# An edge matrix counted in blocks of 32 destinations and a quarter of the sources, in place of 64 and a half

## The chip, the cores and the metric

The kernel runs on one core of a Trainium2 chip. The metric is the device time of one launch in microseconds (us), the median of several runs.

## What is computed

A graph has N = 6250 nodes with 128 features, and E = 100,000 edges (`src`, `dst`, one of 8 types), sorted by `dst`. Two graph networks follow each other, each with its input added and a layer norm behind it:

```python
# three relational layers: messages by edge type, mean over each (node, type)
seg = dst * R + etype
agg = segment_sum(h[src, etype] / max(cnt[seg], 1), dst)
x = agg + x @ root + bias            # then batch norm and relu, but for the last
# then a light graph network on the same edges (row = src, col = dst)
h = x @ W_in + b_in
edge_weight = deg_inv_sqrt[row] * deg_inv_sqrt[col]
for _ in range(3):
    cur = segment_sum(cur[col] * edge_weight[:, None], row)
    acc = acc + cur
final = (acc / 4) @ W_out + b_out
```

The second network needs, three times, the product of the matrix A (how many edges lead from each source to each destination) with a 6250 x 64 matrix. A does not depend on features, so the kernel counts it while the relational layers run.

## The kernel before, in words

**The first network.** For each layer l the kernel makes a table `h_d` of transformed nodes (L975, L976, L977) and walks the edges in tiles of 128. One tile of one layer is a *slot*: POOL gathers 128 rows by an indirect DMA (L1857, out of `x_d` for 100 tiles and out of `h_d` for 462), and PE multiplies them with a small one-hot block (L1860) into a bank that DVE adds to `agg` (L1908) or `z` (L1878). There are `SLOTS` = 562 slots in a layer. A gather has 19 buffers. Destinations with very many edges go another way, `dense` (L1510, L1514, with their loads at L1381 and L1401 and their unpacking at L1423 and L1425).

**What sets the order.** All work beside the slots is written as Python generators. `streams` gives each generator a stretch of slots, and at each slot every stream is advanced in proportion: it emits its instructions until its next `yield`. The order of PE and DVE is taken as emitted (`tc.manual_schedule`); each engine runs its own list in order and waits by semaphores. SP issues nearly all the DMAs, in its own order. In layer 0 run the counts of the busiest destinations (`hot_counts`), `dense` and, from slot 300 to 502, `tables`; in layers 1 and 2 run `dense`, `degrees` and one half each of `counts`.

**Tables.** The edge tiles lie in a grid of 98 rows by 8 tiles. A *step* takes TS = 4 neighbouring tiles (a half row) and one *block* of BD = 64 destinations. Since edges are sorted, each half row is used by one block or by a few neighbouring ones, so there are NST = 196 + 98 = 294 steps for any input. `tables` finds out which block and which half row each step has: comparisons of the blocks' edges with the first and last destination of each half row (L1613, L1615), their sums by matmul (L1623, L1632), masks over all steps (L1639 to L1644), five fp32 matmuls of 294 columns that spread the results over the partitions (L1660), and sixteen that select the steps' sources and destinations (L1675). The tables `e_src`, `rel_s`, `e_val` (128 x 1176, fp32) hold for each edge of each step its column, its row and its value. `step_i` holds the block of each step and whether it is the block's last; `keep` is 0 at a block's first step.

**Counts.** S = 896 sources of seven *fields* share one int32 word by different bits (e_val is a power of two per field), so A needs 896 words a destination. The upper half of these columns is put on other partitions: the 128 partitions of a sum are 64 destinations x 2 halves, with SH = 448 columns each. For every step, over 4 yields and with the matmuls 6 yields behind,
- DVE makes one one-hot block `dst_hot` of 4 x 128 columns (L1732, three buffers),
- DVE makes for each tile a `row` of 448 columns, which holds the edge's value at its column (L1736),
- PE sums `dst_hot` x `row` over the four tiles in one PSUM bank (L1742),
- DVE adds it to the running sum of the block, `had` (L1714, four buffers),
- SP reads block and last-flag into registers, eight steps at a time (L1718), and stores `had` into `a_d` if the step is the block's last (L1723, a conditional DMA of 224 KB, `[block][partition][column]`).

**The last stage** (from about 2710 us) loads `a_d` back (L2109), unpacks the fields with DVE (L2117, L2120) and multiplies with PE (L2128, 7203 matmuls of 193 columns).

Of the kernel before, what the change touches and what calls it, by code (L numbers as in the profile page):

```python
# [17 lines left out]
P = 128  # L18
EPS = 1e-5
REGS = 8  # L20
# [499 lines left out]
def sorted_path(  # L520
# [93 lines left out]
    TS = 4  # L614
    BD = P // 2
    NBD = NP // BD
    SH = S // 2
    FAR = 1 << 14
    NG4 = Q * J // TS
    NST = NG4 + NBD  # L620
    LEAD = 6
# [9 lines left out]
    assert 3 * PART + SUB * R + 3 * P <= NP and 9 * SP * R + R * D <= HD * R and CH * 3 * D <= 3 * SUB * R * 2 and 3 * SUB * R <= PART  # L631
# [3 lines left out]
    assert 96 < Q <= P and N + P <= PAD and NBLK % CH == 0 and NBLK == NF * NSL and J == 2 * TS and NST <= 512 and NBD <= P and SR <= SH and LAG < TS  # L635
# [435 lines left out]
    a_d = dram.tile([NBD, P, SH], I32, name="a_d")  # L1071
# [3 lines left out]
    nc.gpsimd.iota(iota_h.rearrange("p (d q) -> p d q", q=2), pattern=[[1, BD], [FAR, 2]], base=0,  # L1075
                   channel_multiplier=0, allow_small_or_imprecise_dtypes=True)
    iota_s = kp.tile([P, NST], F32, name="iota_s")
    nc.gpsimd.iota(iota_s, pattern=[[1, NST]], base=0, channel_multiplier=0,
                   allow_small_or_imprecise_dtypes=True)
    iota_q = kp.tile([P, 1], F32, name="iota_q")  # L1080
    nc.gpsimd.iota(iota_q, pattern=[[0, 1]], base=0, channel_multiplier=2,
# [33 lines left out]
    def near(minus, n):  # L1115

        far = cp.tile([P, TS, P], BF16, name="lo_far")
        hot = cp.tile([P, TS, P], BF16, name="lo_hot", bufs=4)
        for j in range(n):
            nc.scalar.activation(far[:, j, :], iota_f, AF.Abs, bias=minus[:, j : j + 1])  # L1120
        nc.scalar.activation(hot[:, :n, :], far[:, :n, :], AF.Relu, bias=ones[:, 0:1], scale=-1.0)  # L1121
        return hot
# [431 lines left out]
    NGD = -(-NTS // TS)  # L1554

    def degrees():
        DT = 32
        made, summed = [], []
        for y in range(2 * NGD + 4):
            g = y // 2  # L1560
            if y % 2 == 0 and g < NGD:
                t0 = g * TS
                n, k = min(TS, NTS - t0), t0 % DT
# [8 lines left out]
                far = cp.tile([P, TS, NBLK], BF16, name="blk_far", bufs=1)  # L1572
                blk = cp.tile([P, TS, NBLK], BF16, name="blk_hot", bufs=3)
# [28 lines left out]
    step_i = kp.tile([1, 2, NST], I32, name="step_i")  # L1602
    keep = kp.tile([P, NST], F32, name="keep")

    def tables():

        B = NBD
        edge = kp.tile([P, B], F32, name="edge")
        nc.vector.tensor_scalar(edge, iota_f[:, :B], float(BD), None, op0=OP.mult)
        d_in = dst_f[:, 1 : W + 1]  # L1610
        below = flat(e_val)[:Q, : 4 * B].rearrange("p (h k b) -> p h k b", h=2, k=2)
        for h in range(2):
            nc.vector.tensor_scalar(below[:, h, 0], edge[:Q, :], d_in[:, h * 512 + 511 : h * 512 + 512], None,  # L1613
                                    op0=OP.is_gt)
            nc.vector.tensor_scalar(below[:, h, 1], edge[:Q, :], float(BD), d_in[:, h * 512 : h * 512 + 1],  # L1615
                                    op0=OP.add, op1=OP.is_gt)
# [3 lines left out]
        p_t = [ps_w.tile([P, 512], F32, name="pw")[:B, :1] for _ in range(2)]  # L1620
        for h in range(2):
            for k in range(2):
                nc.tensor.matmul(p_t[k], below[:, h, k], ones[:Q, :1], start=(h == 0), stop=(h == 1))  # L1623
        yield
        col = kp.tile([B, 8], F32, name="col")
        t0, n, incl, s0, delta, top = (col[:, i : i + 1] for i in range(6))
        nc.vector.tensor_copy(t0, p_t[0])
        nc.vector.tensor_tensor(n, p_t[1], t0, op=OP.subtract)
        nc.vector.tensor_scalar_max(n, n, 1.0)
        yield  # L1630
        p_i = ps_w.tile([P, 512], F32, name="pw")[:B, :1]
        nc.tensor.matmul(p_i, upto, n, start=True, stop=True)  # L1632
# [5 lines left out]
        past, within, start_, ends = (flat(e_val)[:B, i * NST : (i + 1) * NST] for i in range(4))  # L1638
        nc.vector.tensor_scalar(past, iota_s[:B, :], incl, None, op0=OP.is_ge)  # L1639
        nc.vector.tensor_scalar(within, iota_s[:B, :], s0, None, op0=OP.is_ge)  # L1640
        yield
        nc.vector.tensor_sub(within, within, past)
        nc.vector.tensor_scalar(start_, iota_s[:B, :], s0, None, op0=OP.is_equal)
        nc.vector.tensor_scalar(ends, iota_s[:B, :], top, None, op0=OP.is_equal)  # L1644
        delta_b = kp.tile([B, P], F32, name="delta_b")
        nc.vector.tensor_copy(delta_b, delta.to_broadcast([B, P]))
        step_b = kp.tile([P, NST], F32, name="step_b")
        step_g = kp.tile([P, NST], F32, name="step_g")
        made = (
            (ones[:B, :], past, lambda p: nc.vector.tensor_scalar(step_b, p[:, :NST], float(BD), None, op0=OP.mult)),  # L1650
            (delta_b, within, lambda p: nc.vector.tensor_add(step_g, p[:, :NST], iota_s)),
            (ones[:B, :], start_, lambda p: nc.vector.tensor_scalar(keep, p[:, :NST], -1.0, 1.0, op0=OP.mult,
                                                                    op1=OP.add)),
            (iota_p[:B, :], ends, lambda p: nc.vector.tensor_copy(step_i[:, 0, :], p[:1, :NST])),
            (ones[:B, :1], ends, lambda p: nc.vector.tensor_copy(step_i[:, 1, :], p[:1, :NST])),
        )
        yield
        for of, by, take in made:
            p = ps_w.tile([P, 512], F32, name="pw")
            nc.tensor.matmul(p[: of.shape[1], :NST], of, by, start=True, stop=True)  # L1660
            yield
            take(p)

        sel = [flat(rel_s)[:Q, h * NST : (h + 1) * NST] for h in range(2)]
        for h in range(2):
            nc.vector.tensor_scalar(sel[h], step_g[:Q, :], float(h), iota_q[:Q, :], op0=OP.subtract,
                                    op1=OP.is_equal)
        yield
        e_key = e_src.bitcast(I32)
        for to, of in ((e_key, key_f), (e_rel, d_in)):  # L1670
            for j in range(TS):
                pe = ps_w.tile([P, 512], F32, name="pw")
                for h in range(2):
                    c = h * 512 + j * P
                    nc.tensor.matmul(pe[:, :NST], of[:, c : c + P], sel[h], start=(h == 0), stop=(h == 1))  # L1675
                yield
                nc.vector.tensor_copy(to[:, :, j], pe[:, :NST])
# [22 lines left out]
        nc.vector.tensor_scalar(upper, e_src, float(SH), None, op0=OP.is_ge)  # L1700
        nc.vector.scalar_tensor_tensor(e_src, upper, -float(SH), e_src, op0=OP.mult, op1=OP.add)
# [3 lines left out]
    def counts():  # L1705

        had = ac.tile([P, SH], I32, name="had")
        nc.vector.memset(had, 0)
        at, runs, ending = {}, [had], []
        rows, hots, sums = {}, {}, {}  # L1710

        def leave(s):
            now = ac.tile([P, SH], I32, name="had")
            nc.vector.scalar_tensor_tensor(now, runs.pop(), keep[:, s : s + 1], sums.pop(s)[:, :SH],  # L1714
                                           op0=OP.mult, op1=OP.add)
            if s % REGS == 0:
                for k, top_ in ((0, NBD - 1), (1, 1)):
                    _, v = nc.values_load_multi_w_load_instructions(  # L1718
                        step_i[0:1, k, s : min(s + REGS, NST)], engines=[ET.SP], min_val=0, max_val=top_,
# [7 lines left out]
        for i in range(NST * TS + LEAD + LAG):  # L1727
            s, j = divmod(i, TS)
            if s < NST:
# [484 lines left out]
```

## Time and profile before

| | |
|---|---|
| median of 3 runs | 3420.43 us (3415.64 to 3430.69) |
| profiled execution | 3407.57 us, of which the span of its instructions is 3405.8 us |
| layer 0 | 0 to about 970 us |
| layer 1, first half of the counts | 971 to 1845 us |
| layer 2, second half of the counts | 1859 to 2706 us |
| last stage | 2709 to 3406 us |
| L1742, 1176 matmuls | 433.8 us busy, 352 ns in the median record |
| L1736, 1176 rows | 451.5 us busy, 402 ns in the mean |
| L1732, 294 one-hot blocks | 202.0 us busy, 687 ns in the mean |
| L1714, 294 running sums | 197.6 us busy, 672 ns in the mean |
| tables, on DVE | 588 to 878 us |

The profile is of one execution. *Busy* is the time in which an engine had at least one instruction of the group under way; matmuls overlap, so a matmul's record is longer than the time by which it holds back the next one. PE is the matmul engine, PEld its weight loads, DVE the vector engine, ACT the scalar engine, POOL the one that issues the gathers, SP the one that issues most DMAs. PEclk is the share of full clock that PE was granted. *Idle before* is the engine's idle time just before the instructions of a group, with what ended it. The *chain* is followed back from the last instruction, at each step to what released it or to the instruction before it on its engine. "issue" is time in which the engine waited for nothing that the profile shows.

### The profile page before, as it was taken

The numbers are of one execution on the slowest core, as the hardware profiler recorded it, in microseconds if no ns is written. First come the engines' busy times: TensorE is split into PE (matmuls) and PEld (weight loads), VectorE is DVE, ScalarE is ACT, GpSimd is POOL, SyncE is SP. The second block draws the span as 40 slices with busy tenths as digits, with TensorE's granted clock in tenths as the row PEclk, the third lists the DMA queues.
The fourth block names the chain that finished last, engine by engine and source line by source line (L and its number), as shares of the span: only waits on it lengthen the run. The fifth ranks groups of instructions, "written<-read, shape, count | busy, mean of one in ns | idle before, by whom it ended". The sixth has DMA issues, their size and how long they took to land.

```text
span 3405.8 us, 57451 instructions
## 1 busy us (share of the span) xinstructions
PE 2833.0 (83%) x19147; PEld 2016.1 (59%) x19147; DVE 2301.2 (68%) x6139; ACT 1121.1 (33%) x3086; POOL 1793.6 (53%) x1703
## 2 busy tenths in 40 slices
PE   5876488889859788878875888888888789999998
PEld 3444355555535455555544455555565589999997
DVE  5977787356547786766776567767667695655665
ACT  3565452000025644353443464535354020000000
POOL 4466666677756777676764667777777500000000
PEclk9876589899869889988996999988988799999998
DMA  6433376555547354554553665545555534443331
GB/s 202 181 110 76 96 215 202 205 177 185 184 140 266 110 191 153 171 182 150 172 174 92 234 220 163 189 153 201 167 173 171 159 89 115 115 115 113 111 104 34
DMA packets 378371, 532.85 MB, mean 156 GB/s; under 512 B 99892, under 2 KB 296674, under 8 KB 378064
## 3 DMA queue, kind: packets, MB, share of 16 engines
q1 hardware_dynamic: 315668, 414.87, 36.9%
q0 software_dynamic: 53952, 110.60, 11.3%
q10 hardware_dynamic: 8444, 3.61, 0.4%
q8 instruction: 152, 2.49, 0.3%
q14 instruction: 155, 1.27, 0.1%
HBM read 390.36 MB, written 205.60 MB: 175 GB/s over the span
## 4 chain that ended last, share of the span: by engine, by line
PE 61%; DVE 11%; issue 8%; another core or an unknown queue 2%; DMA 2%; ACT 2%; DVEq 0%; SPq 0%; POOL 0%; ACTq 0%
PE pw L2128 17%; PE pd L1510 14%; PE ps L1860 7%; PE pw L1742 6%; PE pd L975 5%; PE pd L1514 5%; DVE row L1736 2%; PE pw L1457 1%; DVE had L1714 1%; DVE agg L1908 1%; DVE dst_hot L1732 1%; DMA xT<-c_d 1%; PE pw L1540 1%; PE ps L2078 1%
## 5 line engine op out<-in xcount | busy, mean ns | idle before, releaser
L1857 POOL DMA_INDIRECT gt<-h_d,gidx x1386 | 1468.5, 1060 | 637.0 <-issue 276.3
L1510 PE MATMUL pd<-xT,hs 128*128 128x512 fp8e3 x2646 | 970.5, 421 | 68.1 <-issue 50.4
L1860 PEld LDWEIGHTS ps<-o,gt 128*128 128x128 f32 x3372 | 670.8, 215 | 432.2 <-issue 212.2
L1860 PE MATMUL ps<-o,gt 128*128 128x48 f32 (+1 forms) x3372 | 617.8, 271 | 218.4 <-issue 103.1
L2128 PE MATMUL pw<-three,u 128*128 128x193 bf16 x7203 | 613.5, 248 | 11.7 <-DVE three L2045 9.8
L2128 PEld LDWEIGHTS <-u 128*128 128x128 fp8e3 x7203 | 602.8, 98 | 17.4 <-issue 9.8
L1514 PE MATMUL pd<-xT,hs 128*128 128x256 fp8e3 x1764 | 517.0, 293 | 36.8 <-issue 30.4
L1736 DVE TENSOR_SCALAR row<-iota_c,e_tab,e_tab 128x448 bf16<-128x448 int16 x1176 | 451.5, 402 | 77.6 <-remote 24.1
L1510 PEld LDWEIGHTS <-hs 128*128 128x128 bf16 x2646 | 299.1, 118 | 311.7 <-issue 143.2
L1742 PE MATMUL pw<-row,dst_hot 128*128 128x448 bf16 x1176 | 433.8, 381 | 18.6 <-issue 14.9
L1732 DVE TENSOR_TENSOR dst_hot<-iota_h,e_tab 128x512 bf16<-128x512 f32 x294 | 202.0, 687 | 237.4 <-PE ps L1860 83.7
L975 PE MATMUL pd<-w,xT 128*128 128x512 f32 x588 | 300.8, 636 | 25.7 <-issue 24.7
L1857 POOL DMA_INDIRECT gt<-x_d,xidx x200 | 205.3, 1026 | 144.9 <-PE pw L1742 35.5
L1121 ACT ACTIVATE lo_hot<-lo_far,ones 128x512 bf16<-128x512 bf16 (+1 forms) x370 | 225.3, 611 | 148.4 <-PE pw L1277 69.1
L1575 ACT ACTIVATE blk_far<-iota_f,src_blk 128x49 bf16<-128x49 f32 x782 | 211.4, 324 | 157.6 <-DVE src_blk L1567 71.3
L1576 ACT ACTIVATE blk_hot<-blk_far,ones 128x196 bf16<-128x196 bf16 x196 | 88.1, 449 | 511.3 <-PE ps L1860 213.3
L1120 ACT ACTIVATE lo_far<-iota_f,src_lo 128x128 bf16<-128x128 f32 x782 | 254.7, 387 | 0.1
L1514 PEld LDWEIGHTS <-hs 128*128 128x128 bf16 x1764 | 203.4, 115 | 82.1 <-issue 53.3
L976 ACT COPY hs<-pd 128x512 f32<-128x512 f32 x294 | 171.3, 585 | 221.8 <-PE pd L975 114.9
L1742 PEld LDWEIGHTS <-dst_hot 128*128 128x128 bf16 x1176 | 146.1, 125 | 126.8 <-issue 76.3
L2120 DVE TENSOR_SCALAR u<-packed 128x896 int32<-128x896 int32 x147 | 91.5, 622 | 185.1 <-PE pw L2128 182.7
L1714 DVE SCALAR_TENSOR_TENSOR had<-had,keep,pw 128x448 int32<-128x448 int32 x294 | 197.6, 672 | 3.7 <-PE pw L1742 1.4
(405 smaller groups left out, 2912.9 us busy)
## 6 DMA issues: line engine op xcount, KB each, us to landing
xT<-c_d SPq DMA_DIRECT2D x126, 896.0 KB
h_d<-hs SPq DMA_DIRECT2D x147, 512.0 KB
hs<-p_d SPq DMA_DIRECT2D x105, 672.0 KB
a_d<-had SPq DMA_DIRECT2D x294, 224.0 KB
packed<-a_d SPq DMA_DIRECT2D x147, 448.0 KB
c_d<-had SPq DMA_DIRECT2D x174, 196.0 KB
gt<-h_d,gidx POOLq DMA_INDIRECT x1386
p_d<-hs SPq DMA_DIRECT2D x21, 672.0 KB
```

Source lines behind the costliest of these rows:

```text
L975: nc.tensor.matmul(ph, xT[:, b * P : (b + 1) * P], w[:, c : c + 512], start=True, stop=True)
L1120: nc.scalar.activation(far[:, j, :], iota_f, AF.Abs, bias=minus[:, j : j + 1])
L1121: nc.scalar.activation(hot[:, :n, :], far[:, :n, :], AF.Relu, bias=ones[:, 0:1], scale=-1.0)
L1510: nc.tensor.matmul(sums[0], x3s[n_][:, b, p, :], of[:, :, b, :, :2].rearrange("p s r y -> p y s r"), start=first_, stop=last)
L1514: nc.tensor.matmul(sums[1][:, :HALF], x3s[n_][:, b, p, :], of[:, :, b, :, 2], start=first_, stop=last)
L1714: nc.vector.scalar_tensor_tensor(now, runs.pop(), keep[:, s : s + 1], sums.pop(s)[:, :SH], op0=OP.mult, op1=OP.add)
L1732: nc.vector.tensor_tensor(hots[s], iota_h[:, None, :].to_broadcast([P, TS, P]), rel_s[:, s, :, None].to_broadcast([P, TS, P]), op=OP.is_equal)
L1736: nc.vector.tensor_scalar(rows[i], iota_c, e_src[:, s, j : j + 1], e_val[:, s, j : j + 1], op0=OP.is_equal, op1=OP.mult)
L1742: nc.tensor.matmul(sums[s][:, :SH], hots[s][:, j, :], rows.pop(i - LEAD), start=(j == 0), stop=(j == TS - 1))
L1857: nc.gpsimd.indirect_dma_start(out=gt, out_offset=None, in_=table, in_offset=bass.IndirectOffsetOnAxis(ap=at[:, t : t + 1], axis=0))
L1860: nc.tensor.matmul(pa, gt, columns(t), start=first_, stop=last)
L2128: nc.tensor.matmul(out_of(f), bytes_[WHERE[f][0]][:, d, :, WHERE[f][1]], cur[:, order[c0 + d], :], start=(c0 + d == 0 and f == f0), stop=( ...
```

## The change

A step takes TS = 2 tiles instead of 4, and a block BD = 32 destinations instead of 64. The 128 partitions of a sum are 32 destinations x 4 quarters of the 896 columns, with SQ = 224 columns each. So NG4 = 392, NBD = 196, and NST = 588 steps of two tiles: the tiles of all steps stay 1176. TQ = 4 tiles, that is two steps, share one one-hot instruction and one PSUM bank (2 x 224 columns); each step has its own running sum, conditional store and flags. [...] `a_d` becomes `[196][128][224]`; its words lie where they lay before. `iota_s` has 294 columns, buffers of `row` and `had` keep their size, and 224 of their columns are used. `near` and `degrees` use TQ in place of TS and stay as they are.

```diff
-    TS = 4
-    BD = P // 2
+    TQ = 4
+    TS = 2
+    BD = P // 4
     NBD = NP // BD
+    NBG = NBD // 2
     SH = S // 2
+    SQ = S // 4
     NG4 = Q * J // TS
     NST = NG4 + NBD
+    NSH = NST // 2
+    NSUP = NST * TS // TQ
...
-    a_d = dram.tile([NBD, P, SH], I32, name="a_d")
+    a_d = dram.tile([NBD, P, SQ], I32, name="a_d")
...
-    nc.gpsimd.iota(iota_h.rearrange("p (d q) -> p d q", q=2), pattern=[[1, BD], [FAR, 2]], base=0,
+    nc.gpsimd.iota(iota_h.rearrange("p (d q) -> p d q", q=4), pattern=[[1, BD], [FAR, 4]], base=0,
...
     def tables():
-        B = NBD
+        B, PER = NBG, W // (TS * P)
...
+        for g in range(2):
+            past, within, start_, ends = masks[g]
+            one = lambda v: v[:, g : g + 1]
+            nc.vector.tensor_scalar(past, many[:B], one(incl), None, op0=OP.is_ge)
+            nc.vector.tensor_scalar(within, many[:B], one(s0), None, op0=OP.is_ge)
+            nc.vector.tensor_scalar(start_, many[:B], one(s0), None, op0=OP.is_equal)
+            yield
+            nc.vector.tensor_sub(within, within, past)
+            nc.vector.tensor_scalar(ends, many[:B], one(top), None, op0=OP.is_equal)
+            nc.vector.tensor_copy(delta_b[:, g], one(delta).to_broadcast([B, P]))
+            yield
...
         for of, by, take in made:
-            p = ps_w.tile([P, 512], F32, name="pw")
-            nc.tensor.matmul(p[: of.shape[1], :NST], of, by, start=True, stop=True)
-            yield
-            take(p)
+            for c in (slice(0, NSH), slice(NSH, NST)):
+                p = ps_w.tile([P, 512], F32, name="pw")
+                for g in range(2):
+                    nc.tensor.matmul(p[: of[g].shape[1], :NSH], of[g], masks[g][by][:, c], start=(g == 0),
+                                     stop=(g == 1))
+                yield
+                take(p, c)
...
             for j in range(TS):
-                pe = ps_w.tile([P, 512], F32, name="pw")
-                for h in range(2):
-                    c = h * 512 + j * P
-                    nc.tensor.matmul(pe[:, :NST], of[:, c : c + P], sel[h], start=(h == 0), stop=(h == 1))
-                yield
-                nc.vector.tensor_copy(to[:, :, j], pe[:, :NST])
+                for half in (slice(0, NSH), slice(NSH, NST)):
+                    pe = ps_w.tile([P, 512], F32, name="pw")
+                    for h in range(PER):
+                        c = h * TS * P + j * P
+                        nc.tensor.matmul(pe[:, :NSH], of[:, c : c + P], sel[h][:, half], start=(h == 0),
+                                         stop=(h == PER - 1))
+                    yield
+                    nc.vector.tensor_copy(to[:, half, j], pe[:, :NSH])
...
     def counts():
-        def leave(s):
-            now = ac.tile([P, SH], I32, name="had")
-            nc.vector.scalar_tensor_tensor(now, runs.pop(), keep[:, s : s + 1], sums.pop(s)[:, :SH],
-                                           op0=OP.mult, op1=OP.add)
+        def leave(s, of):
+            now = ac.tile([P, SH], I32, name="had")[:, :SQ]
+            nc.vector.scalar_tensor_tensor(now, runs.pop(), keep[:, s : s + 1], of, op0=OP.mult, op1=OP.add)
...
-        for i in range(NST * TS + LEAD + LAG):
-            s, j = divmod(i, TS)
-            if s < NST:
+        for i in range(NSUP * TQ + LEAD + LAG):
+            s, j = divmod(i, TQ)
+            if s < NSUP:
                 if j == 0:
-                    hots[s] = cp.tile([P, TS, P], BF16, name="dst_hot", bufs=3)
-                    nc.vector.tensor_tensor(hots[s], iota_h[:, None, :].to_broadcast([P, TS, P]),
-                                            rel_s[:, s, :, None].to_broadcast([P, TS, P]),
-                                            op=OP.is_equal)
-                rows[i] = rp.tile([P, SH], BF16, name="row")
-                nc.vector.tensor_scalar(rows[i], iota_c, e_src[:, s, j : j + 1], e_val[:, s, j : j + 1],
+                    hots[s] = cp.tile([P, TQ, P], BF16, name="dst_hot", bufs=3)
+                    nc.vector.tensor_tensor(hots[s], iota_h[:, None, :].to_broadcast([P, TQ, P]),
+                                            rel_s_[:, i : i + TQ, None].to_broadcast([P, TQ, P]), op=OP.is_equal)
+                rows[i] = rp.tile([P, SH], BF16, name="row")[:, :SQ]
+                nc.vector.tensor_scalar(rows[i], iota_c[:, :SQ], e_src_[:, i : i + 1], e_val_[:, i : i + 1],
                                         op0=OP.is_equal, op1=OP.mult)
...
-                nc.tensor.matmul(sums[s][:, :SH], hots[s][:, j, :], rows.pop(i - LEAD), start=(j == 0),
-                                 stop=(j == TS - 1))
+                    sums[s] = ps_w.tile([P, 512], F32, name="pw")[:, : TQ // TS * SQ].rearrange("p (u c) -> p u c", c=SQ)
+                nc.tensor.matmul(sums[s][:, j // TS], hots[s][:, j, :], rows.pop(i - LEAD), start=(j % TS == 0),
+                                 stop=(j % TS == TS - 1))
...
-            if ending and (i - LEAD - LAG) % TS == TS - 1:
-                ending.pop(0)()
+            if ending and (i - LEAD - LAG) % TQ == TQ - 1:
+                s = ending.pop(0)
+                of = sums.pop(s)
+                for u in range(TQ // TS):
+                    leave(s * (TQ // TS) + u, of[:, u])
```

## The prediction

> **What bounds the kernel now.** I read the page's totals first, then the chain of work that ended last, then a table by stage, because the change touches only two stretches of the span: the tables of layer 0 (588 to 878 us) and the counts beside layers 1 and 2 (971 to 1845 and 1859 to 2706 us, the first and last start of L1742 and of the gathers around it).
>
> ```profile
> span 3405.8 us, 57451 instructions
> ...
> PE 2833.0 (83%) x19147; PEld 2016.1 (59%) x19147; DVE 2301.2 (68%) x6139; ACT 1121.1 (33%) x3086; POOL 1793.6 (53%) x1703
> ...
> PE 61%; DVE 11%; issue 8%; another core or an unknown queue 2%; DMA 2%; ACT 2%; DVEq 0%; SPq 0%; POOL 0%; ACTq 0%
> PE pw L2128 17%; PE pd L1510 14%; PE ps L1860 7%; PE pw L1742 6%; PE pd L975 5%; PE pd L1514 5%; DVE row L1736 2%; PE pw L1457 1%; DVE had L1714 1%; DVE agg L1908 1%; DVE dst_hot L1732 1%; DMA xT<-c_d 1%; PE pw L1540 1%; PE ps L2078 1%
> ```
>
> The chain is PE's for 61% and DVE's for 11%. L1742, the matmul that counts edges, holds 6% of it. The table by stage says how full the engines are where it runs:
>
> ```profile
> core 0: us, PE busy (x) PEld busy (x) DVE busy (x) ACT busy (x) POOL busy (x), PEclk, DMA share, GB/s
> 560.00:885.00 325.00, 287.52 (x1679) 182.37 (x1679) 175.30 (x401) 5.61 (x15) 234.54 (x218) 0.92 0.58 194
> 971.00:1845.00 874.00, 709.74 (x3939) 448.48 (x3940) 619.64 (x1618) 398.25 (x1171) 596.94 (x563) 0.89 0.49 164
> 1859.00:2706.00 847.00, 718.09 (x3991) 454.44 (x3992) 577.78 (x1507) 367.62 (x1069) 593.67 (x562) 0.90 0.55 182
> ```
>
> In both layers PE is busy 81 to 85%, DVE 68 to 71%, POOL 68 to 70%; POOL's gathers carry another 0.30 us of issue each, which makes its 562 gathers about 765 us of 874. So PE leads, POOL has some 10% left, and DVE is next. The order of PE and DVE is written by hand and a one-hot block has three buffers, so DVE may run only about three yields ahead of PE: of DVE's waits in layer 1 the largest is that of the one-hots for L1742.
>
> ```profile
> DVE dst_hot L1732 <- PE pw L1742: 49.9, 27, 3.8
> DVE dst_hot L1732 <- PE ps L1860: 28.1, 17, 5.5
> ```
>
> (us in total, times, longest.) DVE waits for PE more than PE for DVE: PE is the bound, with DVE close behind it.
>
> **PE: 1176 matmuls of 448 columns become 1176 of 224.** A record's length is no price, since matmuls overlap; the distance between starts is.
>
> ```profile
> 1399.89 0.28 PE L1514 MATMUL pd<-xT,hs 128*128 128x256 fp8e3 x1
> 1400.01 0.39 PE L1510 MATMUL pd<-xT,hs 128*128 128x512 fp8e3 x1
> ...
> 1400.24 0.35 PE L1742 MATMUL pw<-row,dst_hot 128*128 128x448 bf16 x1
> ...
> 1400.43 0.32 PE L1860 MATMUL ps<-o,gt 128*128 128x48 f32 x2
> ```
>
> 448 columns hold PE 0.19 us though the record says 0.35; 512 hold it 0.23 and 256 0.12. In the whole trace the median distance after an L1742 is 189 ns, and about 370 ns in the half-clock stretches (13% of them). 224 columns would be about 100 ns, between the 256 of L1514 (116) and the 193 of L2128 (175.56 us for 2097, or 84 ns). But 1000 of the 1176 are followed by the fp32 weight load of an L1860, and where no long matmul covers such a load the next start is 112 ns off (after L1860 itself). So I take 110 ns: 79 ns saved of 189, or 42%; at half clock 370 becomes about 214, the same share. The trace gives L1742 264 us of starts to starts (each capped at 450 ns): at most about 110 us go. What matters is its share of the chain: 10.3% of 874 and 12.4% of 847 us, 195 us. 42% of that is **-81 us**.
>
> [...]
>
> **DVE.** The page's groups, mean ns of one behind the busy time:
>
> ```profile
> L1736 DVE TENSOR_SCALAR row<-iota_c,e_tab,e_tab 128x448 bf16<-128x448 int16 x1176 | 451.5, 402 | 77.6 <-remote 24.1 <-PE pw L1742 22.8 <-PE ps L1860 22.1
> ...
> L1732 DVE TENSOR_TENSOR dst_hot<-iota_h,e_tab 128x512 bf16<-128x512 f32 x294 | 202.0, 687 | 237.4 <-PE ps L1860 83.7
> ...
> L1714 DVE SCALAR_TENSOR_TENSOR had<-had,keep,pw 128x448 int32<-128x448 int32 x294 | 197.6, 672 | 3.7 <-PE pw L1742 1.4
> ```
>
> Rows: the same instruction at 392 columns (L1268) has a median of 376 ns, at 448 of 391: 0.27 ns a column, the rest fixed. 224 columns save 60 ns, 1176 x 60 = 70 us; a 256-column row with one scalar fewer (L1348, 280 ns) bounds the saving at about 115 ns, and nothing bounds it below. The running sum: 392 columns take 615 (L1282), 448 take 672, so 224 take about 444 ns, twice as often: 588 x 0.444 - 197.6 = +63 us. The one-hot instruction stays as it is, 294 of 512 columns. **DVE's load is unchanged, -7 us**: the change spends on sums what it saves on rows. On the chain rows have 54 + 25 us and sums 24 + 14 (the same two layers): -15% is -12, +32% is +12. Together 0.
>
> **SP** issues 588 conditional stores of 112 KB instead of 294 of 224 KB (a_d holds the same bytes in the same order, so L2109 reads as before), and 148 register loads of step_i instead of 74. Those loads now take 89 us, and a store with its register work 0.56 us; so SP gets about 255 us more beside some 360 us of own work in 1721. It mostly waits for DVE's sums (272.6 us at L1723) and is off the chain. But SP also issues L1381's loads of c_d, L1401's of p_d and L977's h_d stores, behind these; a load behind a pair and its two register loads starts 2 to 4 us later. The cover is one chunk of look-ahead; xT<-c_d is already 1% of the chain. I put +2 us, bounds 0 and 30 (the 26 us that L1425 waits for it now, once more).
>
> **Tables in layer 0.** 16 fp32 matmuls of 294 columns (L1675) become 32, 5 (L1660) become 20; one is two rows of 249 ns, so 31 x 0.5 = 15.5 us, and the 14 more one-column matmuls of 4 to 18 add about 2. PE has 75% of the chain there: +13 us, at most +18; below, 0, if PE's 37 us of idle took it. DVE gets some 12 us in a stretch where it is busy 54%: nothing.
>
> **Sum.** Of the 80 us on the chain I let a quarter not arrive: a shorter PE step leaves PE waiting for DVE, whose load stays, and for the handovers between the two; and a less busy PE gets a slower clock. -60 + 2 + 13 = -45 us on the profiled 3407.6 us, about 3362. That run lies 13 us below the median of the runs, 3420.4; from the median it would be 3375. I forecast **3360** with 3330 to 3395 as this case's own range.
>
> **Rivals.**
> 1. More arrives: all 110 us of PE's occupancy, and the 16% of PE's idle time that scales with it shrinks too: -125 + 15, about 3300. For it: DVE waits mainly for PE. Against: POOL's 765 us and DVE's unchanged 600.
> 2. DVE takes the bound. If rows stay at 402 ns (their time is mostly fixed) and every sum of the pair lies on the chain, +63 us stand against -81, with +15 of tables and SP: about 3405, no change. For it: PE idles up to 7.8 us at a time for rows in layer 1; two sums stand together in DVE's queue ahead of the next rows and agg additions. Against: 71% busy.
> 3. Slower: the clock. Granted clock follows PE's busy share in the rows: 0.92 at 84 to 87% busy (1300 to 1500, 560 to 830 us), 0.82 at 69% (1700 to 1845), 0.72 at 68% (240 to 560). PE's part of the chain in both layers is about 60% of 1721, 1030 us at 0.895. If halved matmuls push the share under 70% and the clock to 0.82, they cost 9%, +94 us, all other terms -65: about 3435. It decides below a clock of about 0.84. Against: the span shrinks with the work, so PE's share falls only from 83 to about 80%. The longest idle time of PE before an L1742 in layer 1 is 1.0 us (seven in all, 5.3 us). [...]
> 4. The ring of four had buffers turns twice as fast. In layer 0, where four steps take 9.5 us, L1282 waited 23.3 us for c_d<-had in 174 steps; two pairs take 11.7 us here. Some 20 to 40 us: 3380 to 3400.
>
> **How the numbers follow.** Forecast 0.48, rival 1 0.15, rival 2 0.17, rival 3 0.12, rival 4 0.08. The range reaches from rival 1 to just above no change, 3295 to 3425; above it lies rival 3. A measurement of this kernel tells 0.5% (17 us) from no change. Faster by over 0.5%: the forecast, rival 1 and most of 4, 0.70; within 0.5%: rival 2 and the rest of 4, 0.18; slower: 0.12.
>
> **What would show it.** Right: L1742's successor starting about 110 ns after it, rows near 340 ns, sums near 445 ns x588, layers 1 and 2 together 55 to 65 us shorter, tables' stretch 10 to 15 longer, the last stage unchanged. Wrong: rows at 400; waits of L1860 or L1742 for had doubled; had waiting for a_d; PEclk under 0.85 in the two layers; L1425 or L1510 waiting for SP's loads.

## The result, and the profile after

The changed kernel took 3430.0 us (median of 8 runs, 3420.5 to 3436.2) and the kernel before, beside it, 3417.7 us (8 runs): a ratio of **1.0043, 95% interval 1.0025 to 1.0062**. Forecast were 3360 us, with 3295 to 3425 as range. Two later comparisons of the same pair gave 1.0051 [1.0032, 1.0070] and 1.0051 [1.0029, 1.0073]. The change costs some 12 to 19 us where it was to bring 45.

The kernel before itself came out at two levels, 3415 to 3445 us in four of the eight comparisons (the forecast's own among them) and 3140 to 3142 us in the other four, so every ratio here is that of a kernel's time to the kernel before's in the same comparison.

The totals and the chain of the changed kernel's page:

```profile
span 3426.7 us, 60100 instructions
...
PE 2790.7 (81%) x19237; PEld 1978.1 (58%) x19237; DVE 2302.3 (67%) x6457; ACT 1122.0 (33%) x3086; POOL 1783.4 (52%) x1703
...
PE 60%; DVE 10%; issue 8%; another core or an unknown queue 4%; ACT 2%; DMA 1%; DVEq 0%; SPq 0%; ACTq 0%
PE pw L2165 17%; PE pd L1515 15%; PE ps L1897 8%; PE pd L1519 5%; PE pd L980 4%; PE pw L1776 3%; DVE row L1770 2%; DVE had L1750 1%; PE pw L1462 1%; DVE dst_hot L1767 1%; DVE agg L1945 1%; PE pw L1545 1%; PE pd L1588 1%; PE ps L2115 1%
```

The counting matmul (L1742 before, L1776 now) went from 6% to 3% of the chain, and the span grew by 20.9 us. PE is less busy by 42 us and the others are busier by no more than 1.1 us each: the difference is waiting. The table by stage (us of the stage, busy us of PE, PEld, DVE, ACT and POOL with their instructions, granted clock, DMA share, GB/s) has the tables of layer 0, layer 1 and layer 2:

```profile
560.00:885.00 325.00, 300.30 (x1775) 190.94 (x1774) 185.11 (x417) 5.61 (x15) 237.32 (x219) 0.96 0.60 195
966.00:1850.00 884.00, 681.79 (x3939) 424.14 (x3940) 615.18 (x1767) 398.73 (x1171) 596.73 (x563) 0.85 0.51 163
1868.00:2722.00 854.00, 685.70 (x3987) 426.02 (x3988) 573.82 (x1648) 367.34 (x1069) 586.76 (x561) 0.86 0.56 179
```

Beside the three rows in the prediction: the tables' stretch has 12.8 us more of PE's work and the layer ends no later; the two layers lost 60 us of PE's work and gained 17 us of length, and their clock fell from 0.89 and 0.90 to 0.85 and 0.86.

The instructions themselves cost what was forecast. Two groups of DVE (busy us, mean ns | idle before):

```profile
L1770 DVE TENSOR_SCALAR row<-iota_c,e_tab,e_tab 128x224 bf16<-128x224 int16 x1176 | 387.2, 354 | 103.0 <-PE ps L1897 37.3
...
L1750 DVE SCALAR_TENSOR_TENSOR had<-had,keep,pw 128x224 int32<-128x224 int32 x588 | 260.8, 444 | 16.5 <-issue 2.8
```

and PE in the timeline (start us, length us):

```profile
1401.09 0.28 PE L1519 MATMUL pd<-xT,hs 128*128 128x256 fp8e3 x1
...
1401.21 0.26 PE L1776 MATMUL pw<-row,dst_hot 128*128 128x224 bf16 x1
...
1401.30 0.33 PE L1897 MATMUL ps<-o,gt 128*128 128x48 f32 x2
...
1401.47 0.39 PE L1515 MATMUL pd<-xT,hs 128*128 128x512 fp8e3 x1
```

The successor starts 0.09 us after L1776 (median 95 ns at whole clock, 189 before), and the first of its two fp32 rows lasts 58 ns to the next start where it lasted 43. The pair is some 79 ns shorter, the very saving of the forecast, which had put it all into the first distance.

**Where the time went.** Between the first and the last counting matmul the trace before has 1716.7 us and the trace after 1737.6. Split by whether PE works (matmul or weight load) or idles: PE's work 1429.9 to 1371.7 us (-58), its idle time 286.8 to 365.9 (+79). Of the idle time, gaps that end with DVE went from 82.9 to 124.9 us, with ACT from 9.1 to 42.6, gaps ahead of an instruction that waits for nothing from 79.6 to 99.8, and the rest fell. PE's largest wait for DVE, and DVE's two largest for PE, in the whole trace (us, times, longest), before:

```profile
PE ps L1860 <- DVE agg L1908: 47.8, 18, 6.7
```

```profile
DVE dst_hot L1732 <- PE ps L1860: 83.7, 40, 14.5
DVE dst_hot L1732 <- PE pw L1742: 77.9, 49, 3.9
```

and after:

```profile
PE ps L1897 <- DVE agg L1945: 72.5, 27, 11.3
```

```profile
DVE dst_hot L1767 <- PE ps L1897: 76.6, 40, 5.9
DVE dst_hot L1767 <- PE pw L1776: 69.1, 38, 14.1
```

PE waits more for DVE, although DVE has no more to do; DVE's two largest waits for PE fall a little (161.6 to 145.7 us).

### The profile page after: what moved, and what is told of

Read it like the earlier page. It is cut to its first block, busy times and chain, and to the rows that moved or that the text cites. A ratio compares the mean times of both kernels' runs of the same rounds, so it can differ in the third digit from the quotient of the medians.

```text
span 3426.7 us, 60100 instructions
## 1 busy us (share of the span) xinstructions
PE 2790.7 (81%) x19237; PEld 1978.1 (58%) x19237; DVE 2302.3 (67%) x6457; ACT 1122.0 (33%) x3086; POOL 1783.4 (52%) x1703
## 4 chain that ended last, share of the span: by engine, by line
PE 60%; DVE 10%; issue 8%; another core or an unknown queue 4%; ACT 2%; DMA 1%; DVEq 0%; SPq 0%; ACTq 0%
PE pw L2165 17%; PE pd L1515 15%; PE ps L1897 8%; PE pd L1519 5%; PE pd L980 4%; PE pw L1776 3%; DVE row L1770 2%; DVE had L1750 1%; PE pw L1462 1%; DVE dst_hot L1767 1%; DVE agg L1945 1%; PE pw L1545 1%; PE pd L1588 1%; PE ps L2115 1%
## 5 line engine op out<-in xcount | busy, mean ns | idle before, releaser
L1515 PE MATMUL pd<-xT,hs 128*128 128x512 fp8e3 x2646 | 984.4, 426 | 76.5 <-issue 58.2
L1897 PEld LDWEIGHTS ps<-o,gt 128*128 128x128 f32 x3372 | 610.5, 221 | 433.9 <-issue 216.7
L1897 PE MATMUL ps<-o,gt 128*128 128x48 f32 (+1 forms) x3372 | 634.1, 281 | 219.3 <-issue 98.6
L1770 DVE TENSOR_SCALAR row<-iota_c,e_tab,e_tab 128x224 bf16<-128x224 int16 x1176 | 387.2, 354 | 103.0 <-PE ps L1897 37.3
L1776 PE MATMUL pw<-row,dst_hot 128*128 128x224 bf16 x1176 | 317.8, 282 | 28.3 <-issue 13.9
L1750 DVE SCALAR_TENSOR_TENSOR had<-had,keep,pw 128x224 int32<-128x224 int32 x588 | 260.8, 444 | 16.5 <-issue 2.8
L1776 PEld LDWEIGHTS <-dst_hot 128*128 128x128 bf16 x1176 | 150.2, 129 | 130.3 <-issue 80.2
```

The source lines that it names most:

```text
L1515: nc.tensor.matmul(sums[0], x3s[n_][:, b, p, :], of[:, :, b, :, :2].rearrange("p s r y -> p y s r"), start=first_, stop=last)
L1770: nc.vector.tensor_scalar(rows[i], iota_c[:, :SQ], e_src_[:, i : i + 1], e_val_[:, i : i + 1], op0=OP.is_equal, op1=OP.mult)
L1776: nc.tensor.matmul(sums[s][:, j // TS], hots[s][:, j, :], rows.pop(i - LEAD), start=(j % TS == 0), stop=(j % TS == TS - 1))
L1897: nc.tensor.matmul(pa, gt, columns(t), start=first_, stop=last)
```

## What is left to explain, and the theories

- **D**: DVE has no room. What is taken from PE is taken from a chain on which DVE's rows, one-hots and sums stand close behind.
- **S**: SP's doubled register loads and stores delay what is queued behind them.
- **P**: the gathers' pitch on POOL is a floor (1.25 us a slot: the median distance between the starts of gathers in layers 1 and 2 of the trace before, and 99% of them are 1.24 us or more).
- **I**: instructions arrive late. This came out of the trace and not of the forecast: at the higher level PE and SP have pauses of about 0.7 us ahead of single instructions that wait for nothing. The weight loads of the kernel before, in order of time, with the idle time ahead of each:

```profile
2109.98 0.38 PEld L1860 LDWEIGHTS ps<-o,gt 128*128 128x128 f32 x2
2110.83 0.10 PEld L1510 LDWEIGHTS <-hs 128*128 128x128 bf16 x1 [0.48 <-issue]
2111.55 0.10 PEld L1514 LDWEIGHTS <-hs 128*128 128x128 bf16 x1 [0.62 <-issue]
2112.29 0.10 PEld L1510 LDWEIGHTS <-hs 128*128 128x128 bf16 x1 [0.65 <-issue]
2113.02 0.10 PEld L1514 LDWEIGHTS <-hs 128*128 128x128 bf16 x1 [0.63 <-issue]
2113.73 0.10 PEld L1510 LDWEIGHTS <-hs 128*128 128x128 bf16 x1 [0.61 <-issue]
```

For 4 us every weight load comes 0.7 us after the one before; SP's instructions start 0.7 us apart at the same time; ACT and POOL have no such pause in the whole trace. The kernel before has 184 gaps of PE of over 200 ns of this kind (91 us; called late gaps below), the changed one 225 (116 us); SP has 123 and 246 pauses of 500 to 800 ns. At the lower level none of the ten traces has one on either engine.

## Experiments, first comparison: SP, PE and DVE apart

All four fell on the lower level (kernel before 3142.2 us). The edits, of which the main lines are shown: free stores (e1; no register is loaded, and a_d is stored at fixed steps, so it does not hold the matrix),

```diff
-            if s % REGS == 0:
...
-            apart("a", nc.sync.dma_start(a_d[bass.ds(at[0, s], 1), :, :].rearrange("b p c -> p b c"),
-                                         now[:, None, :], cond=(at[1, s] == 1)))
+            b = s * NBD // NST
+            if (s + 1) * NBD // NST > b:
+                apart("a", nc.sync.dma_start(a_d[b : b + 1, :, :].rearrange("b p c -> p b c"), now[:, None, :]))
```

SP's work twice in the kernel before (e2; the register loads are doubled in the same way),

```diff
+            apart("a2", nc.sync.dma_start(a2_d[bass.ds(at[2, s], 1), :, :].rearrange("b p c -> p b c"),
+                                          now[:, None, : SH // 2], cond=(at[3, s] == 1)))
```

half the matmul in the kernel before (e3; the sums read the 224 counted columns twice),

```diff
-                nc.tensor.matmul(sums[s][:, :SH], hots[s][:, j, :], rows.pop(i - LEAD), start=(j == 0),
+                nc.tensor.matmul(sums[s][:, : SH // 2], hots[s][:, j, :], rows.pop(i - LEAD)[:, : SH // 2], start=(j == 0),
...
```

and one sum of 448 columns for a pair of steps in the changed kernel (e4; both steps take the first one's `keep`):

```diff
+            if s % 2 == 0:
+                both = ac.tile([P, SH], I32, name="had")
+                nc.vector.scalar_tensor_tensor(both, runs.pop(), keep[:, s : s + 1], of, op0=OP.mult, op1=OP.add)
...
```

> The changed kernel with SP's part of the counts nearly taken away: no register loads, no conditions, 196 stores of 112 KB to fixed blocks (as many bytes as before; the matrix that is counted is wrong, and its check against the degrees is cleared). Theory S (SP's doubled work, 255 us more in its queue, delays the loads that stand behind the stores, and so takes back what PE gained): 60 to 80 us below the changed kernel, about 3355 us. Rival H (PE and DVE hold each other up in small handovers and DVE's load did not fall, so PE's gain cannot arrive whatever SP does): within 15 us of the changed kernel, 3415 to 3435.

Measured: 3143.6 us, 1.0005 [0.9989, 1.0020].

> The kernel before, with every register load and every conditional store done twice on SP, the second store of half the columns to a place of its own; nothing else changed. Theory S: 40 to 80 us above the kernel before, 3460 to 3500. Rival H: 0 to 15 us above, 3418 to 3433.

Measured: 3145.7 us, 1.0014 [0.9999, 1.0030].

> The kernel before with only the matmul cut to 224 columns; rows, sums (which read the 224 columns twice) and SP's work stay as before, so half of the matrix is wrong and its check is cleared. Theory S: PE's gain arrives, 60 to 80 us below the kernel before, about 3350. Rival H: no more than 15 us below, 3403 to 3418.

Measured: 3135.4 us, 0.9988 [0.9971, 1.0005].

> The changed kernel with one running sum of 448 columns for the two steps of a pair in place of two of 224 (DVE has 63 us less; the sums of half of the steps take the other step's keep, so the matrix is wrong and its check is cleared); stores and register loads as in the changed kernel. Theory S: 0 to 15 us below the changed kernel, 3415 to 3430. Rival H, with DVE as the engine that holds: 40 to 65 us below, 3365 to 3390.

Measured: 3138.8 us, 0.9996 [0.9977, 1.0014].

None of the four moves the time by more than 0.14%. Why is read from PE's waits (us, times, longest), in the kernel before with SP's work twice and in the one with half the matmul:

```profile
PE ps L1868 <- DMA gt<-h_d,gidx: 153.9, 145, 3.4
```

```profile
PE ps L1862 <- DMA gt<-h_d,gidx: 208.4, 189, 3.6
```

At the lower level PE waits for the gathers themselves, and with its matmul cut it waits for them longer: 193 to 214 us at this line in the six such kernels with 224 columns (e1, e3, e4, e9, e11, e18), 154 to 175 us in the four with 448 (e2, e10, e12, e17). That is theory P, at this level; it is read from the waits, and no run here halves the gathers there. In layers 1 and 2 of the trace that the forecast was made from, PE began with 99% of the gathered tiles 8 us or more after they had landed, so there P is not the answer.

## Second comparison: the changed kernel, free stores, half the gathers

This one fell on the higher level (before 3444.5 us). Half the gathers, in either kernel (the second tile of a pair takes the first one's rows):

```diff
+        gt = held.pop(t, None)
+        if gt is None:
+            gt = gp.tile([P, D], F32, name="gt")
...
+            if t % 2 == 0 and t + 1 not in (HT, NTS):
+                held[t + 1] = gt
```

> The changed kernel itself, beside the kernel before on one chip. In the first comparison PE had 184 gaps of over 200 ns ahead of an instruction that waits for nothing (91.2 us) in the kernel before and 225 (115.9 us) in the changed one; SP had 123 and 246 gaps of 500 to 800 ns. On the chip of the first four experiments neither engine had one, and the kernel before was 275 us faster. Theory I (late instructions): the changed kernel is slower only where such gaps are; where there are none, the gathers' pitch on POOL (1.25 us) holds both kernels, and the ratio is 0.996 to 1.002; where the kernel before is near 3420 us, it is 1.002 to 1.006. Theory H (handovers between PE and DVE keep what PE saves, on any chip): 1.002 to 1.006 on both kinds of chip.

Measured: 3456.9 us, 1.0051 [1.0032, 1.0070].

> The first experiment's kernel once more, on the same chip as the changed kernel: the 588 stores with a condition and their 1176 register loads are replaced by 196 plain stores, and no register is loaded for them. Theory I, on a chip with late instructions on SP (168 gaps, some 113 us, in layers 1 and 2 of the changed kernel, 46, some 31 us, in the kernel before): 20 to 50 us faster than the changed kernel. Where there are no such gaps: within 6 us of it. Theory H: within 6 us of it on either.

Measured: 3431.1 us, 0.9970 [0.9955, 0.9985]: 25.8 us below the changed kernel in the same comparison. So SP's work does cost time here, and at the lower level, where its instructions come without pauses, it does not (e1, 1.0005; e2, 1.0014). SP's pauses of 500 to 800 ns fell from 254 to 88. PE's late gaps went from 242 (125 us) to 205 (102 us), which is no more than they differ between two traces of the changed kernel (189, 101 us, in e13).

> The kernel before with every second gather left out; the two tiles' sums take the same gathered rows. POOL then needs some 0.63 us a slot in place of 1.25. Where the gathers hold the kernel (PE waited for them 202.4 us and 153.9 us in the layers of the second experiment's chip) the time falls by 60 to 150 us, to PE's own work. Where the kernel before is near 3420 us, PE starts on each gathered tile 8 us or more after it landed, and the time falls by less than 40 us.

Measured: 2960.8 us, 0.8611 [0.8592, 0.8630]. The expectation failed by far. With half the gathers 484 us go, far more than their pitch, and PE's late gaps nearly all with them (3 remain, 2.2 us in all; SP keeps 19 of its pauses).

> The changed kernel with the same half of the gathers left out. Theory P (the gathers' pitch on POOL hid what PE saves): 50 to 100 us faster than the kernel before with half its gathers, the 81 us that were forecast for PE. Theory H (the handovers with DVE take it back): within 20 us of the kernel before with half its gathers.

Measured: 2957.6 us, 0.8589 [0.8567, 0.8610]: 3.2 us below e7, within the spread of the runs. Neither the pitch nor PE's late gaps (2 are left) stand in the way here, and the change still brings nothing. P and I are not needed for that, and D offers itself. The granted clock is 0.938 to 0.941 in the runs of e7 and 0.924 to 0.932 in those of e8, so it takes a part here too. The chain by engine, first of e7 and then of e8:

```profile
PE 63%; DVE 13%; DMA 3%; issue 3%; ACT 2%; another core or an unknown queue 1%; DVEq 0%; SPq 0%; ACTq 0%
```

```profile
PE 56%; DVE 19%; issue 5%; DMA 2%; ACT 2%; DVEq 1%; SPq 0%; POOL 0%; ACTq 0%; POOLq 0%
```

In layers 1 and 2 the counting matmul's part of the chain falls from 163 to 62 us and that of L1510 and L1514 by 142 us more, while rows go from 81 to 127, one-hots from 38 to 78 and sums from 39 to 90. The place where it shows is PE's wait for the addition that frees its bank, which stands in DVE's queue behind rows and sums; e7, then e8:

```profile
PE ps L1866 <- DVE agg L1914: 53.4, 23, 6.4
```

```profile
PE ps L1903 <- DVE agg L1951: 88.4, 39, 6.9
```

## Third comparison: the parts once more

It too fell on the lower level (before 3140.2 us). e12 is the kernel before with e1's edit.

> The third experiment's kernel once more (the kernel before, its counting matmul cut to 224 of 448 columns; DVE, SP and the steps as they were), for a chip on which PE and SP get instructions late. There the forecast's step (81 us of PE's time taken from the chain) gives 3444 less 60 to 80 us, a ratio of 0.977 to 0.983. Theory D (DVE has no room: when PE is ready earlier it waits for DVE's rows, one-hots and sums): 0 to 25 us less, a ratio of 0.993 to 1.0. Where the kernel before is near 3140 us the gathers' pitch holds it, and the ratio is 0.997 to 1.001 as it was.

Measured: 3135.6 us, 0.9985 [0.9974, 0.9996].

> The second experiment's kernel once more (every register load and store of a_d in the kernel before made twice; the second stores half the bytes). Theory S (SP's doubled work is what the changed kernel pays with late instructions; taking all of it away gave 26 us): on such a chip 12 to 35 us slower than the kernel before, a ratio of 1.003 to 1.010. If SP's work cost nothing there: 0.999 to 1.002. Where the kernel before is near 3140 us: 0.999 to 1.003 as before.

Measured: 3137.9 us, 0.9995 [0.9981, 1.0010].

> The fourth experiment's kernel once more (the changed kernel with one running sum of 448 columns for a pair of steps, so that DVE has 294 sums of 672 ns in place of 588 of 444 ns, 63 us less; SP's stores as in the changed kernel). With late instructions, theory D: 20 to 60 us faster than the changed kernel (1.005 of the kernel before), a ratio of 0.988 to 0.999. If DVE had room: 1.002 to 1.007. Where the kernel before is near 3140 us: 0.997 to 1.002 as it was.

Measured: 3137.0 us, 0.9985 [0.9971, 0.9999].

> The kernel before with its 294 stores with a condition and their 588 register loads replaced by 98 plain stores. With late instructions, theory S: SP's work is half as much as in the changed kernel, so half as much comes back, 8 to 18 us faster than the kernel before (0.995 to 0.998). If only the doubled work hurts, the first half fitting in SP's idle time: within 5 us. Where the kernel before is near 3140 us: 0.998 to 1.002.

Measured: 3138.5 us, 0.9995 [0.9984, 1.0005].

All four stand within 0.15% of the kernel before and tell nothing of the higher level. PE waits 201.8 us for gathers in e9, 208.5 in e11 and 174.8 in e12.

## Fourth comparison: D against the handovers, with half the gathers

The kernel before stood at 3415.0 us.

> The changed kernel once more. Where the kernel before is near 3140 us (no late instructions, the gathers' pitch holds the layers) theory I gives a ratio of 0.997 to 1.002; where it is near 3440 us, 1.003 to 1.007 as twice before.

Measured: 3434.1 us, 1.0051 [1.0029, 1.0073].

> The kernel before with every second gather left out and its counting matmul cut to 224 of 448 columns; DVE's and SP's work as in the kernel before. Its neighbours: 2960.8 us (the kernel before with half its gathers) and 2957.6 us (the changed kernel with half). Theory D (DVE's work is what the chain runs into): 2930 to 2960 us. Theory PE (the cut is worth its 81 us once the gathers are out of the way, and the changed kernel loses it to its doubled sums and stores): 2875 to 2905 us.

Measured: 2925.3 us, 0.8571 [0.8548, 0.8594].

> The changed kernel with every second gather left out and one running sum of 448 columns for a pair of steps: 63 us less of DVE's work than in the changed kernel with half its gathers (2957.6 us); PE's and SP's work as there. Theory D: 2905 to 2935 us. If the handovers hold it, whatever DVE's work: 2945 to 2965 us.

Measured: 2903.4 us, 0.8492 [0.8467, 0.8517].

e14 is just below the range of D and 20 us above that of its rival, and e15 just below that of D. Their neighbours e7 and e8 stand in another comparison, whose kernel before was 0.9% slower, so the size of a step depends on the measure. By the ratios, cutting PE's matmul alone (e7 to e14) takes 0.40%, 14 us of the 81 forecast, and taking 63 us of DVE's work out of the changed kernel (e8 to e15) takes 0.97%, 33 us. By the stretch of the counts in one trace each (1397.4 us in e7, 1386.8 in e8, 1359.8 in e14, 1334.8 in e15) it is 38 and 52 us, but that stretch also differs by 19 us between two traces of the changed kernel itself in these two comparisons (e5 and e13). Within one comparison, e15 is 21.9 us faster than e14: PE's cut is the same, DVE has 64 us less of rows, and SP's work is doubled. By each measure a microsecond of DVE is worth more than one of PE, with the gathers out of the way. e15's chain:

```profile
PE 66%; DVE 11%; issue 3%; DMA 2%; ACT 1%; DVEq 0%; another core or an unknown queue 0%; SPq 0%; POOLq 0%; ACTq 0%
```

DVE is back to 11% and PE up to 66%: in these kernels, whichever of the two is cut, the other takes its place.

## Three more, one by one

> The kernel before with its counting matmul cut to 224 of 448 columns, once more, for a chip with late instructions. Where the kernel before is near 3430 us: by the forecast's step 60 to 80 us less, a ratio of 0.977 to 0.983; by theory D (DVE's work and the late instructions take PE's place) 0 to 30 us less, 0.991 to 1.0. Where it is near 3140 us: 0.997 to 1.000 as twice before.

Measured at the higher level (before 3417.4 us): 3422.5 us, **1.0011** [0.9992, 1.0029]. This is the forecast's main step by itself, and it is worth nothing. The granted clock is 0.865 to 0.874 in these runs and 0.882 to 0.895 in those of the kernel before beside them. The stage of the counts (columns as in the tables by stage):

```profile
995.00:2716.00 1721.00, 1363.21 (x7937) 844.51 (x7936) 1202.09 (x3126) 768.37 (x2242) 1171.09 (x1114) 0.86 0.53 173
```

PE's waits for DVE's additions, and DVE's for the counting matmul:

```profile
PE ps L1862 <- DVE agg L1910: 87.2, 33, 11.1
```

```profile
DVE dst_hot L1734 <- PE pw L1744: 88.4, 43, 13.7
```

PE works 58 us less than before in that stage and idles 62 us more (286.8 to 349.3 us; gaps that end with DVE 82.9 to 128.0). On the chain the matmul goes from 195 to 104 us, and the rest of the chain grows by 96 us in small pieces: rows +13, sums +9, one-hots +8, L1860 +23, waits without a visible releaser +28, and others.

> The kernel before with every register load and store of a_d made twice (the second stores half the bytes), once more, for a chip with late instructions. Cutting PE's matmul alone moved nothing there (1.0011), and the changed kernel stands at 1.0051; if SP's doubled work is the rest: a ratio of 1.003 to 1.007, 10 to 24 us more. If SP's work costs nothing beside late instructions and the split sums are the rest: 0.998 to 1.002. Where the kernel before is near 3140 us: 0.999 to 1.002 as twice before.

Measured at the lower level (before 3141.8 us): 3145.1 us, 1.0019 [1.0007, 1.0031], 3 us.

> The changed kernel with one running sum of 448 columns for a pair of steps (294 sums in place of 588; SP's stores and loads stay doubled), once more, for a chip with late instructions, where the changed kernel stood at 1.0043, 1.0051 and 1.0051 of the kernel before. Theory D: 15 to 50 us less than the changed kernel, a ratio of 0.990 to 1.0007. If SP's doubled work is what is left: 1.003 to 1.007. Where the kernel before is near 3140 us: 0.998 to 1.000 as twice before.

Measured at the lower level (before 3141.6 us): 3135.9 us, 0.9991 [0.9978, 1.0003].

Both missed the level that they were meant for. So the doubling of SP's work alone was not measured where instructions come late, nor the split sums with all gathers there. An estimate fits, but shows nothing by itself: if half of e6's 25.8 us belongs to the half of SP's work that the change adds, 13 us or 0.4% on top of e16's 1.0011 make 1.0049, and 1.0043 to 1.0051 were measured. e16's interval alone is 6 us to either side, so some microseconds may as well belong to the split sums, the rows or the tables.

## Why the prediction was wrong, point by point

- **PE, 81 us on the chain**: right in size. L1742's 195.7 us of the chain became 114.6. That it fits to the microsecond is luck: the same matmul holds 104 to 108 us in the traces of e16, e5 and e13.
- **The step that failed**: "Of the 80 us on the chain I let a quarter not arrive". All of it did not arrive (e16: +0.1%). A share of the chain is what one line holds, not what its removal frees. In e16's stage of the counts the matmul leaves 91 us of the chain; some 32 us come back as slower work of PE, and PE idles 62 us more, 45 of them in gaps that end with DVE. The forecast had named both takers and put them at 20 us together. With the gathers out of the way (e14), 14 to 38 us of 81 came.
- **The clock** was the first of two takers. Rival 3 had its mechanism and set its beginning too low ("It decides below a clock of about 0.84"); it came at 0.85 to 0.86, with PE's busy share down from 81 and 85% in the two layers to 77 and 80%. The trace's clock is either whole or half, in pieces of 3.41 us or multiples; in the stage of the counts the half clock holds 365 us before, 489 after and 473 in e16, and PE works 286, 351 and 349 us within it. L1742 and its successor take 231 ns at whole clock and 454 at half; if all of PE's work slows like that, 65 us more at half speed are 32 us of work more, an estimate: with them the 91 us that the shorter matmuls give become about the 58 that are seen. The clock falls in every comparison with the matmul's cut (0.910 to 0.920 in e3's runs, 0.924 to 0.932 beside them) and not with SP's work doubled (e2, 0.924 to 0.931).
- **DVE's load is unchanged**: right (-64 us of rows, +63 of sums). What was drawn from it was wrong. An engine busy 71% took back part of the gain: PE's gaps that end with DVE grew from 82.9 to 124.9 us, and to 128.0 in e16. That is rival 2's mechanism, not for its reason, since rows did fall to 354 ns on the mean. This was the second taker. On the chain it shows in e16 and with half the gathers (e8), but not in the changed kernel with all of them, where DVE's share is 10% after 11%.
- **SP, +2 us with 0 to 30 as bounds**: by the estimate above too low where instructions come late (13 us, and 26 measured for all of SP's work, within the bounds), about right where they do not (e2, e10, e17: -0.05% to +0.2%).
- **Tables, +13 us**: the work came (287.5 to 300.3 us of PE), the time did not; layer 1 began 5 us earlier.
- **Rival 4**: no. `had` waited 1.9 us for a_d, in two waits.
- **Rival 1**: no. Its "For" (DVE waits mainly for PE) is right as a reading, but it was taken to mean that PE alone led; PE waited for DVE as well, 47.8 us at one line and 82.9 us in the stage of the counts.
- **What was not seen at all**: the 91 us of PE's late gaps stood in the trace as "issue", in which no wait ends. They do not shrink with PE's work (109 us in e16); rival 1 let the idle time shrink.

## What stays open

What sets the level is not known. It is not the chip, since chips 13 and 8 each came out at both. At the higher level PE's late gaps all but vanish with half the gathers (1 to 3 are left in e7, e8, e14 and e15, beside 13 to 40 pauses of SP), so nearly all of PE's need the gathers; by what way the gathers delay PE's and SP's instructions was not found. How the change's 12 to 19 us divide between SP's work, the split sums and the tables was not measured, nor why PE's gaps that end with ACT grew from 9.1 to 42.6 us (17.0 in e16). The changed kernel itself never came up at the lower level; its nearest relatives there (e1, e4, e11, e18) stand at 0.9985 to 1.0005. No variant here that does the whole work is faster than the kernel before.

## What to carry to other kernels

A line's share of the chain is not what cutting it gives: here 91 us of it gave nothing (e16), while half the gathers, with POOL at 0% of the chain and DMA at 2%, gave 484 us (e7). Ask of each engine that works in turns with the line how late it would be if the line were gone, and where the engine to be relieved already waits for another (PE for DVE, 82.9 us here), expect that wait to grow. Count the clock's answer as a term: here PE's shorter matmuls, in a span of about the same length, came with more half clock for its other work (365 us of it before, 473 in e16). Before trusting a chain, look at the idle time that ends without a releaser, and take away the work of another engine (here half the gathers) to see what it hides.

## What the runs showed of the hardware

- Single instructions of PE and of SP can come 0.7 us apart with nothing to wait for, in trains of mostly 1 to 4 us (44 trains of two or more late gaps at most 1 us apart on PE in the kernel before, 64 in the changed one), and only at one of two levels that differ by 8 to 10%. The trace before has 152 packets of 16,384 bytes in a DMA queue of the kind "instruction" (q8 of its page); the train shown above lies between two of them, at 2096.0 and 2120.4 us, so these packets do not explain this one.
- The clock is whole or half in all 20 traces (89 pieces of each in the trace before, 93 in the trace after). In the stage of the counts of the kernel before the half clock began 57 times. In the 3.41 us ahead of each beginning (the length of the shortest pieces) PE's matmuls filled 36% at the median and at most 65%.
- At the higher level, half the gathers made the kernel 484 us faster, though the waits of PE's matmuls for gathers of `h_d` made up 4.6 us in all in the trace before, and POOL was busy 53% of the span. In the stage of the counts PE idles 110 us in e7 where it idled 287 before, and works 1288 us where it worked 1430; its work at half clock fell from 286 to 74 us.
